# Edge features of two node groups in one pass of TensorE's two row halves, in a graph network of eight layers on one core

## The chip, the core and the metric

The kernel runs on one core of a Trainium2 chip. A core has five engines with an instruction stream each: TensorE (PE in the profile, with its weight loads as PEld) multiplies matrices into PSUM, VectorE (DVE) and ScalarE (ACT) work element by element and can read and write PSUM, GpSimd (POOL) issues the indirect DMAs that gather and scatter rows, and SyncE (SP) issues most other DMAs. The engines run side by side and wait for each other through semaphores. The metric is the device time of one execution in microseconds (us); lower is better.

## The reference

The graph has 3125 nodes with 256 features and 50000 edges, sorted by receiver `dst`; everything is fp32. Eight layers follow each other, each added onto x: four of them work on the graph, four are feed-forward networks (FFN). The change touches mostly the work that the kernel does in one loop for the first three:

```python
# layer 0, graph: a weight matrix of 256x256 for each of 16 edge types
msg = einsum('ni,rio->rno', layernorm(x), weight)[edge_type, src] * edge_weight1
x = x + segment_sum(msg, dst)
# layer 0, FFN: 8 experts, gelu, weighted by the top 2 of a router; all tokens
x = x + moe(layernorm(x))
# layer 1, graph
cut = 0.5 * (cos(edge_weight * pi / 5) + 1) * (edge_weight < 5)
W   = (edge_attr_64 @ W_dist + b_dist) * cut[:, None]        # 64 -> 256
agg = segment_sum(embed_table[node_type][src] * W, dst)
x = x + concat([layernorm(x), agg]) @ W_comb + b_comb
```

After that come an FFN on the highest-scored rows (layer 1), a graph layer with attention over the edges and an FFN with 16 experts, top 2 (layer 2), and a graph layer with a maximum over the edges and an FFN with 8 experts, top 2 (layer 3).

## The kernel before

**The loop over tiles, `stage_one`.** Receivers are taken in 25 tiles of 126 nodes, a tile in 21 groups of 6 nodes (the last tile in 17), 521 groups in all. As the edges are sorted, the edges of a group are a run of at most 128 consecutive ones, and a group's work has the edges on the 128 partitions. `window(k)` (L874) does one group:

- `rows[k]` holds for each edge the sender's normalized row and its embedding, 512 columns, gathered by POOL (`fetch_rows`, nine buffers `g`).
- Two matmuls sum the first half by node and edge type (L881, into `c`): the right side is `s0`, 128 edges by 96 = 6 nodes x 16 types, one-hot times the edge's weight, built by DVE (L866). ACT copies `c` into `aT` for every second group (L885).
- One matmul makes the edge filter (L888, into `pw`): the left side is `feats[k]`, 65 rows by 128 edges, loaded by SP (`fetch_feats`, a row of ones and the 64 features, from a table laid out that way); the right side `wd` has `b_dist` in row 0 and `W_dist` in the other 64.
- DVE multiplies `pw` with the embedding half of the row (L891) into `mt`. Then the next row gather is issued.

`build` (L859) also makes `s1` (L868): for each edge its receiver's place in the tile as a one-hot, 32 wide or 128 wide, times the cutoff. `add_up(t, b)` (L896) multiplies `s1` with `mt` into `agg`, for three batches of groups: in the first two, four groups at a time go to four blocks of 32 columns of TensorE (L907). Groups run in the order of the batches, so that batch 0 ends with group 17, batch 1 with 19 and batch 2 with 10; batches 0 and 1 are summed a few groups later, batch 2 after the tile's groups.

After the groups a tile has eight steps of `weigh` (L915): in each, `aT` of two edge types times their 256x256 weights, added up in PSUM (`f`); the last adds the result to x. After each group and each `weigh` step comes a slot, `between()` (L1140): it issues one step of the `flows` (the FFN of layer 0 and the rest of layer 1 for a pair of finished tiles), one of the `background`, and one load of late weights (on ACT's DMA queue) and one zero fill (on SP's).

**The background** is a Python generator: each `yield` ends a step. It prepares, beside the loop, tables for it and for later layers. `begin(t)` (L1211) finds where the groups of tiles t and t+1 start among the edges: `find.fetch` gathers rows, and two slots later `starts` (L647) counts in them (DVE, `find.count`, L586) and multiplies the counts (PE, L651). Further on the edge features are reduced to an attention term (`b_at`, L1276, 100 loads), and nodes are ranked by degree, one tile after the other: `chosen(t)` makes a one-hot on DVE (L1325) for matmuls (L1347), a second loop (L1371 to L1377) places the ranked nodes by one-hots `k_sel` and `k_ohh`. Steps of the background are taken in every slot for the first 116 slots, in every third after that.

**Order.** The stages are under `manual_schedule`: each engine takes its instructions in the order in which the program issues them. PSUM in the loop has two banks for `c`, two halves-of-banks `pw`, one each for `agg` and `f`, and two `w` for flows and background.

**The experts of layers 2 and 3** (class `Experts`) are laid out by a planner, `Plan` (L1685): each job is a generator that yields the engine, an estimated duration and what it waits for, and the planner orders the issues by estimated times. `loads` (L1978) is the job of SP's loads: for each chunk of tokens and each expert, first the tokens `x` (two buffers; it waits until the chunk's rows have been scattered, `self.sent`), then the two blocks of weights (rings of `W_BUFS` = 2 buffers). `run` (L1999) does the expert's matmuls. In layer 2 the gathers of the graph layer use nine buffers `g_rows` before.

## Time and profile before

| | us |
|---|---|
| median of 7 runs | 3792.72 |
| lowest and highest run | 3787.91, 3804.38 |
| the profiled execution, its own time | 3798.97 |
| its span, first to last instruction | 3797.3 |
| loop over tiles, `stage_one` | 99 to 1716 |
| layer 2, gathers of the attention layer | 2028 to 2646 |
| layer 2, experts, last chunk | 2684 to 2816 |
| layer 3, gathers | 2880 to 3390 |
| layer 3, experts | 3445 to 3797 |

A page of the profile is of one execution: busy time by engine, the span in 40 slices (each digit the busy share in tenths; PEclk the granted TensorE clock in tenths of full speed), the DMA queues, the chain that ended last, and the costliest groups of instructions. A group's line reads: code line, engine, operation, output<-inputs, shapes, xcount | busy us, mean ns of one | idle time of the engine just before them, and the instructions that ended most of it. A line of waits reads: who waited <- for whom: us in total, times, longest. In a timeline a line stands for several passes of one kind: start, time from the first start to the last end, engine, line, operation, xcount. An fp32 matmul shows as two passes. Tiles of the loop end at 178.0, 271.3, 345.0, 423.9, 480.8, 535.6, ... 1715.7 us; from the fifth on most odd tiles take 54.9 us, tiles 12 and 13 together 188.7.

### The profile page before, as it was taken

What the parts mean: (1) busy time and instruction counts of PE and PEld (TensorE: products, weight loads), DVE (VectorE), ACT (ScalarE), POOL (GpSimd) and SP (SyncE); (2) the same over time, 40 slices, a digit from 0 to 9 for tenths busy, and PEclk for the clock granted to TensorE, in tenths of its full rate; (3) what the DMA queues carried; (4) which work ended last, traced back from release to release, by engine and by line L of the source; (5) the groups of instructions that cost most, each with busy time, mean ns of one, the idle gap of its engine ahead of it and who ended that gap; (6) DMA issues with size and microseconds to landing.
All of it is one profiled execution on the core that took longest, in us unless ns stands there. A gap on an engine that the chain in (4) does not pass through costs nothing. (4 is left out here: it accounts for less than half of the span.)

```text
span 3797.3 us, 46833 instructions
## 1 busy us (share of the span) xinstructions
PE 2632.4 (69%) x13015; PEld 2108.9 (56%) x13015; DVE 1962.7 (52%) x7555; ACT 851.2 (22%) x1821; POOL 1722.2 (45%) x1971
## 2 busy tenths in 40 slices
PE   3778899999899999998492228568562112238994
PEld 2556788877677888886371117356451112226673
DVE  4445666666566555554334665656663333346311
ACT  2112232322122233232120113123230000014331
POOL 0342343352154343320125777777346777753333
PEclk9967999999899999999595559779785555557997
DMA  5756654553243454430213348677543333324563
GB/s 178 235 156 210 179 145 133 155 163 88 68 127 109 115 151 122 116 110 26 92 56 88 103 115 274 178 217 235 169 154 86 105 105 105 105 80 139 158 213 96
DMA packets 274481, 518.32 MB, mean 136 GB/s; under 512 B 53069, under 2 KB 176107, under 8 KB 274195
## 3 DMA queue, kind: packets, MB, share of 16 engines
q0 software_dynamic: 103744, 303.34, 27.3%
q1 hardware_dynamic: 159598, 201.27, 17.4%
q10 hardware_dynamic: 10852, 10.45, 0.9%
q8 instruction: 113, 1.85, 0.2%
q14 instruction: 174, 1.42, 0.1%
HBM read 428.07 MB, written 86.78 MB: 136 GB/s over the span
## 5 line engine op out<-in xcount | busy, mean ns | idle before, releaser
L136 POOL DMA_INDIRECT g<-tab,m_si x521 | 496.3, 953 | 953.0 <-DVE mt L891 503.8
L136 POOL DMA_INDIRECT g_rows<-tab,srcI x413 | 402.9, 976 | 130.9 <-issue 102.7
L136 POOL DMA_INDIRECT g_row<-tab,srcI x413 | 390.7, 946 | 131.3 <-issue 119.7
L881 PEld LDWEIGHTS c<-s,g 128*128 128x128 f32 x2084 | 343.9, 215 | 124.0 <-issue 45.4
L881 PE MATMUL c<-s,g 128*128 128x96 f32 x2084 | 350.7, 296 | 65.0 <-DMA g<-tab,m_si 21.6
L920 PE MATMUL f<-w_rel,aT 128*126 128x256 f32 x1600 | 380.9, 389 | 0.0
L888 PE MATMUL pw<-w_d,f 65*128 65x256 f32 x1042 | 370.2, 440 | 0.0
L885 ACT COPY aT<-c 128x384 f32<-128x384 f32 (+1 forms) x323 | 237.7, 736 | 572.2 <-PE c L881 552.2
L2368 DVE TENSOR_TENSOR ACC<-ACC,g_row 128x256 f32<-128x256 f32 x413 | 175.6, 425 | 340.4 <-DMA g_row<-tab,srcI 340.2
L920 PEld LDWEIGHTS f<-w_rel,aT 128*126 128x126 f32 x1600 | 305.2, 193 | 52.1 <-issue 4.3
L1643 PE MATMUL tp<-ident,ACC 128*128 128x128 f32 x50 | 16.6, 435 | 420.8 <-DVE ACC L2368 420.8
L1973 PE MATMUL mm<-ro_xt,ro_w 128*128 128x192 f32 (+3 forms) x1152 | 268.8, 382 | 48.6 <-ACT ro_h L2038 23.6
L891 DVE TENSOR_TENSOR mt<-pw,g 128x256 f32<-128x256 f32 x521 | 218.2, 419 | 95.7 <-PE pw L888 94.6
L1977 PE MATMUL y<-ro_w,ro_h 128*96 128x256 f32 (+2 forms) x1152 | 265.9, 383 | 0.0
L1973 PEld LDWEIGHTS mm<-ro_xt,ro_w 128*128 128x128 f32 x1152 | 202.5, 208 | 98.2 <-ACT ro_h L2038 32.2
L1643 PEld LDWEIGHTS tp<-ident,ACC 128*128 128x128 f32 x50 | 7.2, 204 | 428.3 <-issue 353.2
L1977 PEld LDWEIGHTS y<-ro_w,ro_h 128*96 128x96 f32 (+2 forms) x1152 | 199.3, 178 | 42.9 <-issue 1.0
L1038 PE MATMUL w<-w,b_h 128*126 128x256 f32 x800 | 217.2, 396 | 5.5 <-ACT xt L951 4.5
L1029 PE MATMUL w<-xt,w 128*128 128x252 f32 (+1 forms) x832 | 212.1, 379 | 3.0 <-ACT b_h L1031 1.3
L2248 DVE SCALAR_TENSOR_TENSOR ACC<-g_rows,g_e,ACC 128x256 f32<-128x256 f32 x413 | 201.2, 487 | 13.6
L1040 DVE SCALAR_TENSOR_TENSOR x<-w,b_comb,x 126x256 f32<-126x256 f32 x200 | 96.0, 480 | 173.4 <-PE w L1038 172.6
L140 POOL DMA_INDIRECT xg<-XX,ro_pos x100 | 101.1, 1011 | 176.5 <-issue 75.4
(582 smaller groups left out, 4623.7 us busy)
## 6 DMA issues: line engine op xcount, KB each, us to landing
ro_w<-in_L_ffn_blocks SPq DMA_DIRECT2D x72, 514.0 KB
ro_w<-in_L_ffn_blocks SPq DMA_DIRECT2D x72, 512.0 KB
f<-in_attr_t SPq DMA_DIRECT2D x521, 32.5 KB
xg<-zero SPq DMA_DIRECT2D x78, 200.0 KB
b_at<-in_edge_attr SPq DMA_DIRECT2D x100, 125.0 KB
tabr<-v SPq DMA_DIRECT2D x12, 758.0 KB
g<-tab,m_si POOLq DMA_INDIRECT x521
g_rows<-tab,srcI POOLq DMA_INDIRECT x413
```

The source lines that it names most:

```text
L136: return nc.gpsimd.indirect_dma_start(out=dst, out_offset=None, in_=table, in_offset=bass.IndirectOffsetOnAxis(ap=idx, axis=0))
L881: nc.tensor.matmul(pc[:, h, o : o + GW], g[:, h * P : (h + 1) * P], sums[k][0], start=True, stop=True)
L885: nc.scalar.copy(aT[:, :, :, b : b + n * GN].rearrange("p k r n -> p k n r"), pc[:, :, : n * GW].rearrange("p k (n r) -> p k n r", r=16))
L888: nc.tensor.matmul(pw, feats.pop(k), wd, start=True, stop=True)
L891: nc.vector.tensor_tensor(mt[0], pw, rows.pop(k)[:, D:], op=OP.mult)
L920: nc.tensor.matmul(cur["f"][:TN], aT[:, h, r, :], wrel[:, h, r, :], start=(r == 0 and h == 0), stop=(r == 15 and h == 1))
L1029: nc.tensor.matmul(ph, w["01"][:, e, k, i * P : (i + 1) * P], xt[:, k, : n * TN], start=(k == 0), stop=(k == 1))
L1038: nc.tensor.matmul(py, last[:, k, i * TN : (i + 1) * TN], w["02"][:, e - 1, k, :], start=(k == 0), stop=(k == 1))
L1973: nc.tensor.matmul(ph, w[:, o : o + P], xt[:, k, :], start=(k == 0), stop=(k == 1))
L1977: nc.tensor.matmul(py, h[:, i, s], w[:, i * D : (i + 1) * D], start=(i == 0), stop=(i == self.fc - 1))
L2248: stt(u, g[:, r, :D], e[:, r0 + r : r0 + r + 1], u, op0=OP.mult, op1=OP.add)
L2368: nc.vector.tensor_tensor(u, u, rows.pop(r), op=OP.max)
```

## The change

- The groups of a tile are taken in pairs, in their order; the last of a tile stands alone. A tile `f` holds the features of two groups, 64 rows each in the two halves of the partitions, and `wd` holds `W_dist` twice. When the second group's `c` is issued, the two filter matmuls follow each other, each with 64 rows of its own half. `F_BUFS` is 4 pairs, no longer 6 groups.
- The bias is `bd`, `b_dist` on all partitions. `seed()` makes ACT copy it into a PSUM bank `pw` (three banks now) ahead of the matmul, which adds to it. The first three seeds are ahead of the loop and have a matmul with the identity as well.
- The cutoff is multiplied in DVE's product, which becomes a `scalar_tensor_tensor`. One-hots without it are made by `whose(t, b)` for a batch at a time: for batches 0 and 1 in two instructions of four groups each (at groups 4 and 15), for batch 2 in five (at group 10, ahead of its `window`).
- `agg` and `f` share one PSUM bank, `af`. The third `add_up` comes in the first slot after the groups; `weigh` takes the other seven, with two or three edge types each.
- In the background, `find.count` has a step of its own ahead of `starts`; the one-hots of the ranking are made one item ahead of PE.
- In `Experts`, `loads` becomes `tokens` and `weights`, two jobs for the planner; in layer 2 the weights of the last chunk's experts from the third on go into the gathers' buffers, after the last of the gathers.
- The path for groups with too many edges (`beyond`) is adapted, and an unused tile (`lg2`) goes. Both are left out below, as are the planner's lines that only carry the new names.

```diff
@@ -86,7 +86,7 @@
-G_BUFS, F_BUFS = 9, 6
+G_BUFS, F_BUFS = 9, 4
@@ -366,7 +366,8 @@
-    wd = wb.tile([65, D], F32, name="w_d")
+    wd = wb.tile([P, D], F32, name="w_d")
+    bd = wb.tile([P, D], F32, name="b_d")
@@ -410,8 +411,9 @@
-    nc.scalar.dma_start(wd[0:1, :], a["L1_gnn_b_dist"])
-    nc.scalar.dma_start(wd[1:65, :], a["L1_gnn_W_dist"])
+    for i in range(2):
+        nc.scalar.dma_start(wd[64 * i : 64 * i + 64, :], a["L1_gnn_W_dist"])
+    nc.scalar.dma_start(bd, bass.AP(tensor=a["L1_gnn_b_dist"].tensor, offset=a["L1_gnn_b_dist"].offset, ap=[[0, P], [1, D]]))
@@ -646,8 +648,6 @@
     def starts(t, n, pf):
-        for i in range(t, t + n):
-            find.count(i)
@@ -673,6 +673,8 @@
+            for t in range(2):
+                find.count(t)
@@ -832,9 +834,17 @@
-        rows, feats, sums = {}, {}, {}
-        agg_of = {}
-        nxt = {"g": 0, "f": 0, "s": 0}
+        pairs, half_of = [], {}
+        for k, (t, j) in enumerate(wins):
+            if pairs and len(pairs[-1]) == 1 and wins[pairs[-1][0]][0] == t:
+                pairs[-1].append(k)
+            else:
+                pairs.append([k])
+            half_of[k] = len(pairs) - 1, len(pairs[-1]) - 1
+        rows, feats, sums, seeds = {}, {}, {}, []
+        nxt = {"g": 0, "f": 0, "s": 0, "d": 0}
@@ -846,12 +856,25 @@
+            if k < len(pairs):
+                nxt["f"] += 1
+                feats[k] = eb.tile([P, P], F32, name="f", bufs=F_BUFS)
+                for i, w_ in enumerate(pairs[k]):
+                    t, j = wins[w_]
+                    v = nc.values_load(mixI[j : j + 1, t : t + 1], engines={EN.SP}, min_val=0, max_val=E)
+                    nc.sync.dma_start(feats[k][64 * i : 64 * i + 64, :], a["attr_t"][:, bass.ds(v, P)])
+        def seed():
+            k = nxt["d"]
             if k < len(wins):
-                nxt["f"] += 1
-                t, j = wins[k]
-                feats[k] = eb.tile([65, P], F32, name="f", bufs=F_BUFS)
-                v = nc.values_load(mixI[j : j + 1, t : t + 1], engines={EN.SP}, min_val=0, max_val=E)
-                nc.sync.dma_start(feats[k], a["attr_t"][:, bass.ds(v, P)])
+                nxt["d"] += 1
+                pw = ps("pw", [P, 2, D])[:, 0, :]
+                if k < 3:
+                    nc.tensor.matmul(pw, ident, bd, start=True, stop=True)
+                nc.scalar.copy(pw, bd)
+                seeds.append(pw)
@@ -860,14 +883,9 @@
-                a = quarter(j)
-                a, m1 = (0, P) if a is None else (32 * a, 32)
-                s1 = eb.tile([P, m1], F32, name=f"s1_{m1}", bufs=13 if m1 == 32 else 3)
-                nc.vector.tensor_scalar(s1, iota_f[:, a : a + m1], m[:, F_DST, j : j + 1], m[:, F_CUT, j : j + 1],
-                                        op0=OP.is_equal, op1=OP.mult)
-                sums[k] = s0, s1
+                sums[k] = s0
@@ -878,33 +896,64 @@
-                nc.tensor.matmul(pc[:, h, o : o + GW], g[:, h * P : (h + 1) * P], sums[k][0], start=True, stop=True)
+                nc.tensor.matmul(pc[:, h, o : o + GW], g[:, h * P : (h + 1) * P], sums[k], start=True, stop=True)
-            pw = ps("pw", [P, D])
-            nc.tensor.matmul(pw, feats.pop(k), wd, start=True, stop=True)
+            del sums[k]
+            q, i = half_of[k]
+            if i + 1 < len(pairs[q]):
+                return
+            ft = feats.pop(q)
+            pws = [seeds.pop(0) for _ in pairs[q]]
+            for i, pw in enumerate(pws):
+                v = slice(64 * i, 64 * i + 64)
+                nc.tensor.matmul(pw, ft[v, :], wd[v, :], start=False, stop=True, skip_group_check=True)
-            mt = mults[t, j] = eb.tile([P, D], F32, name="mt", bufs=11), sums.pop(k)[1]
-            nc.vector.tensor_tensor(mt[0], pw, rows.pop(k)[:, D:], op=OP.mult)
-            fetch_rows()
-        ag_of, mults = {}, {}
+            for k, pw in zip(pairs[q], pws):
+                t, j = wins[k]
+                mt = mults[t, j] = eb.tile([P, D], F32, name="mt", bufs=11)
+                stt(mt, pw, mts[t][:, F_CUT, j : j + 1], rows.pop(k)[:, D:], op0=OP.mult, op1=OP.mult)
+                seed()
+                fetch_rows()
+        ag_of, mults, ones_of = {}, {}, {}
+        def whose(t, b):
+            m = mts[t][:, F_DST]
+            n = GL if t == NT - 1 else GC
+            for js in together[b]:
+                js = [j for j in js if j < n]
+                if b < 2:
+                    s1 = eb.tile([P, 4, 32], F32, name="s1g", bufs=3)
+                    of = m[:, js[0] : js[-1] + 1 : 5].unsqueeze(2).to_broadcast([P, len(js), 32])
+                    nc.vector.tensor_tensor(s1[:, : len(js)], iota_f.rearrange("p (q n) -> p q n", n=32)[:, : len(js)],
+                                            of, op=OP.is_equal)
+                    for i, j in enumerate(js):
+                        ones_of[t, j] = s1[:, i, :]
+                    continue
+                for j in js:
+                    q = quarter(j)
+                    n1 = P if q is None else 32
+                    s1 = ones_of[t, j] = eb.tile([P, n1], F32, name=f"s1_{n1}", bufs=2 if q is None else 3)
+                    o = 32 * (q or 0)
+                    nc.vector.tensor_scalar(s1, iota_f[:, o : o + n1], m[:, j : j + 1], None, op0=OP.is_equal)
         def add_up(t, b):
             if b == 0:
-                cur["agg"] = ps("agg", [P, D])
+                cur["agg"] = ps("af", [P, 2, D])[:, 0, :]
             for js in together[b]:
-                    a = quarter(j)
-                    mt, s1 = mults.pop((t, j))
-                    o = agg if a is None else agg[32 * a : 32 * a + 32]
-                    nc.tensor.matmul(o, s1, mt, start=not begun, stop=(j == 10), skip_group_check=True)
+                    q = quarter(j)
+                    o = agg if q is None else agg[32 * q : 32 * q + 32]
+                    nc.tensor.matmul(o, ones_of.pop((t, j)), mults.pop((t, j)), start=not begun, stop=(j == 10),
+                                     skip_group_check=True)
@@ -913,9 +962,9 @@
-            if i == 0:
-                cur["f"] = ps("f0", [P, D])
-            for r in (2 * i, 2 * i + 1):
+            if i == 1:
+                cur["f"] = ps("af", [P, 2, D])[:, 0, :]
+            for r in range(16 * (i - 1) // 7, 16 * i // 7):
@@ -1152,6 +1201,8 @@
+        for _ in range(3):
+            seed()
@@ -1161,6 +1212,8 @@
+                if wins[k][1] in (4, 15, 10):
+                    whose(t, (4, 15, 10).index(wins[k][1]))
@@ -1180,9 +1233,10 @@
             for i in range(8):
-                weigh(t, i)
-                if i == 1:
+                if i == 0:
+                else:
+                    weigh(t, i)
@@ -1213,6 +1267,9 @@
+            yield
+            for i in range(t, t + n):
+                find.count(i)
@@ -1341,8 +1398,9 @@
+        nxt = chosen(0)
         for t in range(NT):
-            sel = chosen(t)
+            sel, nxt = nxt, (chosen(t + 1) if t + 1 < NT else None)
@@ -1365,15 +1423,21 @@
+        def both(t):
+            ohl = eb.tile([P, P], F32, name="k_sel")
+            ohh = eb.tile([P, 3, NT], F32, name="k_ohh")
+            nc.vector.tensor_scalar(ohl, iota_f, lo[:, t : t + 1], None, op0=OP.is_equal)
+            for i in range(3):
+                nc.vector.tensor_scalar(ohh[:, i, :], iota_f[:, :NT], hi[:, t : t + 1], val[:, t, i : i + 1],
+                                        op0=OP.is_equal, op1=OP.mult)
+            return ohl, ohh
+        nxt = both(0)
+        yield
             for t in range(t0, t0 + 5):
-                ohl = eb.tile([P, P], F32, name="k_sel")
-                ohh = eb.tile([P, 3, NT], F32, name="k_ohh")
-                nc.vector.tensor_scalar(ohl, iota_f, lo[:, t : t + 1], None, op0=OP.is_equal)
-                for i in range(3):
-                    nc.vector.tensor_scalar(ohh[:, i, :], iota_f[:, :NT], hi[:, t : t + 1], val[:, t, i : i + 1],
-                                            op0=OP.is_equal, op1=OP.mult)
+                (ohl, ohh), nxt = nxt, (both(t + 1) if t + 1 < NT else None)
@@ -1423,7 +1487,7 @@
-            tc.tile_pool(name="eb", bufs=2) as eb, psums(c0=2, pw=2, agg=1, f0=1, w=2):
+            tc.tile_pool(name="eb", bufs=2) as eb, psums(c0=2, pw=3, af=1, w=2):
@@ -1976,25 +2040,38 @@
-        def loads(self):
-            pool, half = self.pool, 2 * self.f + self.fc
+        def tokens(self):
-                    r0 = e * m * k
+                    r0, at = e * m * k, c * self.n + e
-                    xfree = self.XR.take()
-                    x = pool.tile([P, self.bk, D], F32, name="ro_x", bufs=2)[:m, :k]
+                    free = self.XR.take()
+                    x = self.pool.tile([P, self.bk, D], F32, name="ro_x", bufs=2)[:m, :k]
-                    parts = [(x, plan[0].moved(f, m * k * 1024), xfree)]
-                    for i, ring in enumerate(self.W):
-                        f = yield "SP", 0.45, (ring,)
-                        wfree = ring.take()
-                        w = pool.tile([P, half if i == 0 else self.fc * D], F32, name=f"ro_w{i}", bufs=W_BUFS)
-                        nc.sync.dma_start(w, self.blocks[e * P : (e + 1) * P, half * i : half + i * self.fc * D])
-                        parts.append((w, plan[0].moved(f, 0.53e6), wfree))
-                    self.there.append(parts)
-                    self.came[len(self.there) - 1].t = f
+                    self.there[at] = x, plan[0].moved(f, m * k * 1024), free
+                    self.came[at].t = f
+        def weights(self, more=None):
+            half = 2 * self.f + self.fc
+            for c in range(len(self.chunks)):
+                for e in range(self.n):
+                    for i in range(2):
+                        n = (half, self.fc * D)[i]
+                        if more and c + 1 == len(self.chunks) and e >= W_BUFS:
+                            ring, make, since = more
+                            f = yield "SP", 0.45, (ring, since)
+                            w = make()[:, :n]
+                        else:
+                            ring = self.W[i]
+                            f = yield "SP", 0.45, (ring,)
+                            w = self.pool.tile([P, n], F32, name=f"ro_w{i}", bufs=W_BUFS)
+                        free = ring.take()
+                        nc.sync.dma_start(w, self.blocks[e * P : (e + 1) * P, half * i : half * i + n])
+                        at = (c * self.n + e) * 2 + i
+                        self.loaded[at] = w, plan[0].moved(f, 0.53e6), free
+                        self.fetched[at].t = f
@@ -2306,7 +2386,9 @@
-            pl.add(0, ex2.loads())
+            pl.add(0, ex2.tokens())
+            pl.add(0, ex2.weights((blocks, lambda: gp.tile([P, GB, ZW], F32, name="g_rows", bufs=GR_BUFS)
+                                   .rearrange("p r d -> p (r d)"), here[order2[-1]])))
@@ -2469,9 +2552,8 @@
-    f = np.zeros((65, EPAD), np.float32)
-    f[0, :E] = 1.0
-    f[1:, :E] = given["edge_attr_64"].T
+    f = np.zeros((64, EPAD), np.float32)
+    f[:, :E] = given["edge_attr_64"].T
```

## The prediction

> **What bounds the kernel now.** I read the page's totals and its 40 slices first, then busy time by stretch, then groups, PE's waits and single passes. The page:
>
> ```profile
> span 3797.3 us, 46833 instructions
> PE 2632.4 (69%) x13015; PEld 2108.9 (56%) x13015; DVE 1962.7 (52%) x7555; ACT 851.2 (22%) x1821; POOL 1722.2 (45%) x1971
> PE   3778899999899999998492228568562112238994
> PEclk9967999999899999999595559779785555557997
> ```
>
> A slice is 95 us. PE is full from slice 5 to slice 18 and nearly idle in the gather stages (2028 to 2646, 2880 to 3390 us), which POOL bounds and the change leaves alone. The tile loop is 99 to 1716 us. By stretch (length, then PE, PEld, DVE, ACT and POOL busy, granted clock, DMA share, GB/s):
>
> ```profile
> 178.00:271.00 93.00, 63.98 (x249) 48.53 (x250) 37.26 (x146) 9.91 (x14) 38.49 (x41) 0.60 0.53 151
> 896.00:1085.00 189.00, 172.12 (x853) 138.05 (x853) 113.88 (x508) 35.05 (x64) 48.49 (x51) 0.86 0.28 78
> 1085.00:1716.00 631.00, 613.62 (x3519) 514.66 (x3517) 368.45 (x1529) 187.04 (x349) 235.57 (x272) 0.98 0.43 121
> 2660.00:2680.00 20.00, 7.36 (x23) 4.46 (x23) 12.86 (x71) 2.55 (x7) 1.10 (x3) 0.50 0.00 0
> 2684.00:2816.00 132.00, 104.95 (x547) 86.30 (x548) 87.08 (x320) 47.86 (x138) 56.60 (x71) 0.88 0.65 213
> ```
>
> The reader sees two kinds of time. In 1085 to 1716 PE is 97% busy: only less PE work helps. Elsewhere PE has gaps, and a gap costs twice, as the clock sits near half behind it. The tile loop's gaps are named by PE's waits in 90 to 1720 us (total, times, longest):
>
> ```profile
> PE w L651 <- DVE startF L586: 35.6, 10, 5.7
> PE c L881 <- DMA g<-tab,m_si: 21.6, 1, 21.6
> PE c L881 <- DVE s L866: 19.4, 20, 2.6
> PE w L1377 <- DVE k_ohh L1375: 10.1, 17, 2.6
> ```
>
> **The change part by part.** The sum goes against the profiled execution: 3798.97 us, a span of 3797.3 and 1.7 around it. That is 6.25 us above the median of the runs, 3792.72; I take the sum off both alike.
>
> *Pairs on PE.* Single passes (start, us, instructions), from three stretches:
>
> ```profile
> 1302.51 0.62 PE L888 MATMUL pw<-w_d,f 65*128 65x256 f32 x2
> 1302.97 0.58 PE L881 MATMUL c<-s,g 128*128 128x96 f32 x4
> ...
> 1338.97 0.62 PE L888 MATMUL pw<-w_d,f 65*128 65x256 f32 x2
> 1339.53 1.07 PE L907 MATMUL agg<-mt,s 128*32 128x256 f32 x16
> 1340.53 1.13 PE L1038 MATMUL w<-w,b_h 128*126 128x256 f32 x4
> ...
> 1135.39 1.12 PE L1012 MATMUL w<-w_b,b_ct 8*126 8x256 f32 x4
> 1136.44 0.91 PE L920 MATMUL f<-w_rel,aT 128*126 128x256 f32 x3
> ```
>
> pw costs 1302.97 − 1302.51 = 0.46 us: two passes, 0.23 each. Two of them cost 0.92. L907 shows that parts of the array do work side by side: 16 passes of 32 columns in 1.00 us, where 16 × 0.23 would be 3.7. L1012 shows what a change to few rows and back costs: four passes take 1.05 us, not 4 × 0.216 = 0.86, so 0.19; the pass before it also runs 0.10 long in such places (L888 ahead of L907: 0.56, not 0.46). Together about 0.29 beside the passes, with a first weight load exposed some 0.39. A pair side by side: 2 × 0.216 + 0.39 = 0.82, against 0.92: −0.10 × 248 pairs = −24. A tile's 21 groups leave one unpaired: 0.82 against 0.46, +0.36 × 25 = +9. I take −14. Upper end: the halves run one after the other, 4 × 0.216 + 0.39 = 1.25, +0.33 × 248 + 9 = +91. No row here has two halves of rows, so both ends stay; I side with L907, the only row in which parts of the array meet.
> The Trainium skill (TensorEngine Tiling (Array Packing), section Theoretical Speedup) allows up to 2× at 64 rows; by that alone 248 pairs would save 0.46 each, −114 us, and the sum below would be −171. The same page, section PSUM Bottleneck, speaks against the change: packing speeds up TensorE, not the emptying of PSUM, which here grows by a seed and a longer product a group; were that the limit, the pairs would give nothing and the sum be −57. L891's product, 0.419 us in slots of 1.75, does not show that limit before the change.
>
> *Bias.* 521 copies of 128×256 by ACT into PSUM. Nearest rows: from PSUM 0.37, between SBUF tiles 0.51:
>
> ```profile
> L2055 ACT COPY ro_y<-y 128x256 f32<-128x256 f32 x32 | 11.8, 370 | 35.9 <-PE y L1977 34.6 <-issue 1.3
> L2218 ACT ACTIVATE g_u<-XX,hasnt 128x256 f32<-128x256 f32 x25 | 12.7, 510 | 0.0
> L2248 DVE SCALAR_TENSOR_TENSOR ACC<-g_rows,g_e,ACC 128x256 f32<-128x256 f32 x413 | 201.2, 487 | 13.6
> ```
>
> That is 193 to 266 us on an engine 30% busy in 1085 to 1716; it rises to some 45%. The new wait: ACT holds a seed until DVE has read that bank, and behind it in ACT's order stand the copy of c and the flows' ACT steps. With three banks, a pair's loop is 0.2 + two products 0.98 + a seed 0.5, 1.7 us, against two slots of 1.75 us: covered, at nothing. If the cover goes (ACT behind a DMA issue, or a product late), each pair pays up to some 0.2: +50.
>
> *Cutoff and one-hots, DVE.* Removed: L868, 147.6 + 17.1 = 164.7 us. Added: 100 four-wide comparisons at L1331's 0.295, 30; 74 narrow and 50 wide at 0.313 and 0.343, 40; 521 products 0.487 instead of 0.419, 35. Net −60 us on an engine 58% busy, off the path; it may shorten the 19.4 us of L866's waits, which I leave as a bound. But before group 10's product stand s0 and five one-hots, 1.6 us, and the sum over the last groups moves from after four relations to the first slot, so that PE meets a product not ready: 0 to 0.5 us a tile, and the bank shared by sums and `f` makes the first relations wait for ACT's 0.37 copy, behind a flow step except in the early tiles. +6 (0 to +20). Steady part with the pairs: −14 + 6 = −8. Its ends: −34 (−15 with no stall, and L866's 19.4 gone) and +111 (+91 + 20; the +50 of uncovered seeds is not added there, as a slower PE gives them cover).
>
> *f and wd loads.* SP still issues 521 loads, of 64 rows for 65. One load of bias more on ACT's queue ahead of the loop; nothing. POOL's gathers now leave in twos, nine buffers deep, and POOL waits 503.8 us for buffers already: nothing.
>
> *Background.* `find.count` runs a slot ahead of the matmul in `starts`, so the 35.6 us over ten waits (L651) go; what is late next is the same DVE work behind other PE work, and the edge loads, twelve steps later, fall out of the phase that steps every slot. Also, 178 to 271 us runs at clock 0.60 where PE's work is 64 of 93 us. Fewer gaps help there, but DMA carries half of its time and tile 0's first gathers (21.6) are untouched; ACT's weight loads hold up c's copies by 12.3 us there and now seeds too. Ends: −65 (35.6 and the half-clock share of 30) to +5. I take −28. Thirteen added steps end a sequence that finished at 1214 us, 500 before the loop: nothing. In 896 to 1085 the one-hots made one item ahead remove L1377's 10.1 and its like, and part of the half clock: 17 us of gaps there; −15 (−30 to 0).
>
> *Level-2 and level-3 experts.* In 2660 to 2680 DMA moves 0 GB/s: weights stand in SP's queue behind token loads that wait for the scatter. Split, they are loaded then, and the last chunk uses the idle gather buffers. PE's gaps in 2684 to 2816 are 132 − 105 = 27 us, of which some 21 name weights and tokens; the tokens' own load stays. Next in line are the stores of the outputs and the fixed tail to 2880. −16 (−35 to +5). In the last level the gaps mostly follow routing: −4 (−10 to +5).
>
> Sum: −8 − 28 − 15 − 16 − 4 = −71: 3728 for a profiled execution like this one, 3722 for the median.
>
> **The rivals.**
> *Halves one after the other* (slower). For it: no row shows two row halves together. Against it: L907. Price: +91 in place of −14, with the +6 and the other moves' −63: +34, 3827. It decides from where what the other moves bring is eaten: (63 − 9 − 6)/248, 0.19 us a pair more than two old products.
> *ACT becomes the late engine.* Seeds and products wait for each other and pairs pay 0.2: +50. For it: one in-order ACT queue with DMA issues in it. Against it: 30% busy. −71 + 50: 3772.
> *The gaps close altogether.* 178 to 424 us runs at full clock (−65) and the L2 experts become PE-bound (−35), lookahead −30: −130, 3662 or so. For it: the clock in 424 to 896 is 0.97 wherever PE has no gaps. Against it: the other waits there (gathers, b_at) stay.
> *Nothing that shows.* The background's waits turn into waits on the same DVE work one slot later and the pairs' gain is eaten by unpaired groups: 3793.
>
> **How the numbers follow.** As summed 0.52 (own range 3685 to 3765); gaps closed 0.13; ACT late 0.16; halves in turn 0.13; nothing 0.06. A measurement of this kernel tells about 0.2%, 7.6 us, from no change. Faster: 0.52 + 0.13 + 0.15 of ACT late = 0.80; same: 0.04; slower: 0.13 + 0.03 of nothing = 0.16. The range 3642 to 3812 takes in the first three and part of the fourth, leaving out some 0.15. Predicted: the likeliest, 3722.
>
> **What would show it.** *Pairs:* the step from a pair's first pass to the next c near 0.8 us (side by side) or 1.25 (in turn). *Bias:* the seeds' group near 370 to 510 ns, idle ahead of it named by DVE's product, and no wait of PE on ACT. *One-hots:* L868 gone, DVE down by some 60 us. *Background:* no wait of `starts` on startF, the stretch 178 to 271 shorter by 15 or more. *Lookahead:* tiles 12 and 13, 188.7 us now, near 174. *Experts:* weights on the DMA in 2660 to 2680, the stretch to the end of the experts shorter by 16. The prediction is wrong if odd tiles in 1085 to 1716, 54.9 us now, are longer than 57, or if c waits for ACT's copies.

## The result and the profile after

The changed kernel takes 3805.91 us (median of 15 runs, 3801.57 to 3810.31), beside 3792.05 for the kernel before (36 runs): a ratio of 1.0035, interval 1.0026 to 1.0044. It is 13.9 us slower. Forecast were 3722 us, a gain of 71, with 3642 to 3812 as the range and 0.16 for slower. The time lies inside the range and the direction was wrong. One run of `split_only`, a kernel described below, took 4525.6 us at a granted clock of 0.60; it belongs to a slower state and is left out of that kernel's ratio.

The profiled execution took 3797.28 us, with a span of 3795.4. That is 8.6 us under the median of its kernel, and the profiled execution of before was 6.9 us over its own. Set against each other the two traces show the changed kernel 1.7 us faster, while the runs say 13.9 slower. The traces are used for where time goes, the runs for how much it is.

The page of the changed kernel:

```profile
span 3795.4 us, 46667 instructions
PE 2616.4 (69%) x13021; PEld 2019.7 (53%) x13021; DVE 1923.3 (51%) x7257; ACT 1031.6 (27%) x2343; POOL 1727.8 (46%) x1971
PE   3777899989989999998493228658682112238994
PEclk9867999999989999999596558769685555557997
```

The work moved as reckoned in kind: DVE is 39 us less busy (60 were reckoned from the removed and added lines), ACT 180 more, PE 16 less. The same stretches as before, after the change (length, PE, PEld, DVE, ACT, POOL, granted clock, DMA share, GB/s):

```profile
178.00:271.00 93.00, 64.85 (x285) 46.19 (x286) 39.11 (x155) 22.84 (x44) 41.01 (x44) 0.65 0.58 168
896.00:1085.00 189.00, 169.60 (x894) 130.50 (x894) 119.58 (x509) 56.80 (x121) 55.86 (x59) 0.92 0.35 97
1085.00:1716.00 631.00, 599.27 (x3453) 468.80 (x3452) 359.74 (x1455) 255.49 (x559) 238.02 (x272) 0.98 0.42 118
2660.00:2680.00 20.00, 6.12 (x13) 2.53 (x13) 17.04 (x58) 2.26 (x7) 9.31 (x16) 0.50 0.71 249
2684.00:2816.00 132.00, 106.45 (x547) 85.93 (x547) 89.42 (x346) 49.01 (x140) 59.00 (x74) 0.86 0.50 163
```

DMA now carries 249 GB/s in 2660 to 2680 where it carried none: the weights do come early. But the tile loop ends 12 us later (its last `weigh` matmul at 1727.3, before at 1715.2), and in 1085 to 1716 PE is less busy in the same time. PE's waits in 90 to 1720 us show where it stands:

```profile
PE af L955 <- DVE s1g L933: 36.6, 26, 5.1
PE c L899 <- DVE s L886: 31.1, 33, 4.5
PE w L651 <- DVE startF L588: 30.5, 9, 8.4
PE c L899 <- DMA f<-in_attr_t: 18.8, 1, 18.8
PE af L955 <- DVE s L943: 15.6, 11, 7.5
PE w L1441 <- DVE k_ohh L1431: 10.9, 18, 2.7
PE w L1078 <- ACT xt L1000: 8.2, 9, 1.2
```

Two of these lines are new: the sums (L955) wait 36.6 + 15.6 = 52 us for one-hots, those of four groups (L933) and those of batch 2 (L943). Before, the sums waited 5.9 us in all. And two lines that were to go are still there: `starts` waits 30.5 us (35.6 before), the ranking 10.9 (10.1 before). The wait of `c` for the other one-hots, `s0` (L886), which the prediction hoped to see shorter, has grown from 19.4 to 31.1 us, and the FFN's matmuls wait 9.1 us for a copy by ACT, `xt` (8.2 of them at L1078; 4.1 before).

The tiles' ends (us, with the tile's length), from the last `weigh` matmul of each. The third and fourth pairs of columns are the kernels `bg_only` and `early_onehots`, described below:

```
tile      before          after        bg_only   early_onehots
  3    417.3  75.8    413.3  90.6    394.0  76.0    409.7  85.9
 11    895.8  60.0    899.8  65.8    863.3  61.4    883.5  65.0
 14   1149.2  64.7   1154.0  96.0   1120.9 103.2   1138.9  97.5
 17   1323.7  54.9   1335.7  60.3   1295.4  57.5   1317.5  60.3
 24   1715.2  51.4   1727.3  52.5   1685.9  51.4   1706.1  51.0
```

### The profile page after: what moved, and what is told of

It is laid out like the page before. It is cut to its first block, busy times and chain, and to the rows that moved or that the text cites. A ratio compares the mean times of both kernels' runs of the same rounds, so it can differ in the third digit from the quotient of the medians.

```text
span 3795.4 us, 46667 instructions
## 1 busy us (share of the span) xinstructions
PE 2616.4 (69%) x13021; PEld 2019.7 (53%) x13021; DVE 1923.3 (51%) x7257; ACT 1031.6 (27%) x2343; POOL 1727.8 (46%) x1971
## 5 line engine op out<-in xcount | busy, mean ns | idle before, releaser
L899 PEld LDWEIGHTS c<-s,g 128*128 128x128 f32 x2084 | 315.9, 210 | 126.6 <-issue 55.6
L899 PE MATMUL c<-s,g 128*128 128x96 f32 x2084 | 339.8, 297 | 60.3 <-DVE s L886 31.1
L969 PE MATMUL af<-w_rel,aT 128*126 128x256 f32 x1600 | 370.3, 383 | 6.5 <-ACT ag L962 6.5
L969 PEld LDWEIGHTS af<-w_rel,aT 128*126 128x126 f32 x1600 | 299.6, 189 | 59.9 <-ACT ag L962 13.1
L918 DVE SCALAR_TENSOR_TENSOR mt<-pw,m_mt,g 128x256 f32<-128x256 f32 x521 | 228.3, 477 | 97.4 <-PE pw L913 96.5
L876 ACT COPY pw<-b_d 128x256 f32<-128x256 f32 x521 | 197.1, 383 | 283.5 <-DVE mt L918 273.2
L2037 PE MATMUL mm<-ro_xt,ro_w 128*128 128x192 f32 (+3 forms) x928 | 234.0, 402 | 29.6 <-ACT ro_h L2118 24.1
L2041 PE MATMUL y<-ro_w,ro_h 128*96 128x256 f32 (+2 forms) x1040 | 245.6, 390 | 0.0
L1078 PE MATMUL w<-xt,w 128*128 128x252 f32 (+1 forms) x832 | 219.4, 388 | 11.4 <-ACT xt L1000 8.2
L913 PE MATMUL pw<-w_d,f 64*128 64x256 f32 x1042 | 221.4, 471 | 0.8 <-ACT pw L876 0.8
L2037 PEld LDWEIGHTS mm<-ro_xt,ro_w 128*128 128x128 f32 x928 | 171.7, 207 | 75.1 <-ACT ro_h L2118 30.8
L2041 PEld LDWEIGHTS y<-ro_w,ro_h 128*96 128x96 f32 (+2 forms) x1040 | 182.4, 180 | 42.9 <-issue 1.3
```

What stands on the lines that cost most here:

```text
L876: nc.scalar.copy(pw, bd)
L899: nc.tensor.matmul(pc[:, h, o : o + GW], g[:, h * P : (h + 1) * P], sums[k], start=True, stop=True)
L913: nc.tensor.matmul(pw, ft[v, :], wd[v, :], start=False, stop=True, skip_group_check=True)
L918: stt(mt, pw, mts[t][:, F_CUT, j : j + 1], rows.pop(k)[:, D:], op0=OP.mult, op1=OP.mult)
L969: nc.tensor.matmul(cur["f"][:TN], aT[:, h, r, :], wrel[:, h, r, :], start=(r == 0 and h == 0), stop=(r == 15 and h == 1))
L1078: nc.tensor.matmul(ph, w["01"][:, e, k, i * P : (i + 1) * P], xt[:, k, : n * TN], start=(k == 0), stop=(k == 1))
```

## The experiments

The kernels were run in groups; those of a group share a chip and the runs of before. In the runs of the result and in three groups (chips 12, 9 and 3 of the record) before took 3791 to 3795 us; in two others (chips 8 and 7) it took 4284 and 4254. The first are called the faster chips here, the last two the slower chips. Runs on the slower chips are given with the ratio to their own before and are told apart.

### The three parts alone

Three kernels are the kernel before with one part of the change each: `split_only` has `tokens` and `weights` in place of `loads`; `loop_only` the tile loop's part; `bg_only` the background's two.

> The kernel before with one part of the change alone: the experts' loads split into tokens and weights (and the last chunk's weights in the gathers' buffers). Theory A, that this part gives what the profile after shows between 2646 and 2880 us: 10 to 16 us faster than before, 3776 to 3782. Rival B, that the gain there is an accident of the one profiled execution: within 4 us of 3792.

> The kernel before with the tile loop's part alone: pairs, seeds, cutoff in the product, one-hots by batch, shared bank; background and experts' loads as before. Theory A, that the loop's part costs, since PE waits for one-hots (52 us of waits named in the profile after) against 8 us won on the pairs: 10 to 25 us slower than before, 3802 to 3817. Rival B, that the pairs' gain and the waits cancel and the loss lies in the background's steps: within 5 us of 3792.

> The kernel before with the background's part alone: the count one step ahead and the one-hots of the ranking one item ahead. Theory A, that waits only change their names, as DVE is the late one with the same work: within 8 us of 3792 either way. Rival B, the prediction's sum for these two terms: 43 us faster, 3749. Rival C, that the steps added push later work into denser tiles: 8 to 15 us slower.

Before: 3790.96. `split_only`: 3776.45, ratio 0.9958 (0.9944 to 0.9973), 14.5 us faster. `bg_only`: 3776.47, ratio 0.9957 (0.9942 to 0.9973), also 14.5 faster. `loop_only`: 3824.03, ratio 1.0087 (1.0069 to 1.0105), 33 us slower. So the headline part costs and the two beside it gain. My expectation of nothing for the background was a miss: it gains, though not the 43 us of the prediction. The three sum to +4 us, the whole is +13.9. The 10 us between them are no more than the four intervals leave open (3 to 7 us each way), so that it isn't shown that anything arises only when the parts meet.

### The one-hots

In `own_onehots` each group's one-hot is built by itself two groups ahead, as before the change; in `early_onehots` the batches stay and are only issued earlier:

```diff
-                if wins[k][1] in (4, 15, 10):
-                    whose(t, (4, 15, 10).index(wins[k][1]))
+                if wins[k][1] in (16, 14, 15):
+                    whose(t, (16, 14, 15).index(wins[k][1]))
                 window(k)
```

> The kernel after with each group's receiver one-hot built alone and two groups ahead, as before the change, but without the cutoff; 521 instructions of DVE in place of 174. Theory A, that the batches' late one-hots cost the loop its pairs' gain: 10 to 25 us faster than the kernel after, 3781 to 3796, with the sums' waits on one-hots gone. Rival B, that DVE's time itself is what counts: 40 to 60 us more of DVE work make it 5 to 15 us slower than the kernel after, 3811 to 3821.

> The kernel after with the one-hots of each batch issued three to four groups earlier in DVE's order (batch 0 at the seventh group and no longer the tenth, batch 1 at the fourteenth and no longer the eighteenth, batch 2 at the eighteenth and no longer the last); same instructions. Theory A, that what costs is the slack, one slot between a batch's one-hots and the sum that needs them when DVE stands behind a DMA: at least as fast as with one-hots of each group, 3778 to 3790. Rival B, that the bunches themselves cost: 3800 to 3808.

`own_onehots`: 3788.23, ratio 0.9992 (0.998 to 1.0004), 17.7 us under the changed kernel. `early_onehots`: 3767.72 against a before of 3792.29, ratio 0.993 (0.9907 to 0.9952), 38.2 us under the changed kernel with the same instructions. That settles the largest cause: not the number of the one-hots, their place. What the 20 us between the two kernels are is not settled: `own_onehots` has 297 instructions more on DVE (521 one-hots in place of 224; the 174 of its expectation is a miscount), 37 us of busy time in the traces. PE's waits in `early_onehots`, the same view:

```profile
PE c L899 <- DVE s L886: 35.6, 35, 4.0
PE w L651 <- DVE startF L588: 31.1, 9, 8.0
PE c L899 <- DMA f<-in_attr_t: 18.7, 1, 18.7
PE af L955 <- DVE mt L918: 10.3, 6, 6.8
```

The sums' waits on one-hots are gone; 10.3 us on products are left. How a one-hot can come to be late shows in the timeline of the changed kernel around 376 us (start, us, instruction, idle before and what ended it). VectorE:

```profile
374.63 0.87 DVE L918 SCALAR_TENSOR_TENSOR mt<-pw,m_mt,g 128x256 f32<-128x256 f32 x2
377.47 0.42 DVE L1333 TENSOR_TENSOR b_at<-b_at,b_a 125x256 f32<-125x256 f32 x1 [1.97 <-DMA b_at<-in_edge_attr]
...
380.73 0.42 DVE L1333 TENSOR_TENSOR b_at<-b_at,b_a 125x256 f32<-125x256 f32 x1 [2.14 <-DMA b_at<-in_edge_attr]
...
381.76 0.49 DVE L933 TENSOR_TENSOR s1g<-iota_f,m_mt 128x128 f32<-128x128 f32 x2
382.16 0.87 DVE L918 SCALAR_TENSOR_TENSOR mt<-pw,m_mt,g 128x256 f32<-128x256 f32 x2
```

and TensorE:

```profile
375.88 1.23 PE L913 MATMUL pw<-w_d,f 64*128 64x256 f32 x4
382.10 1.94 PE L955 MATMUL af<-mt,s1g 128*32 128x256 f32 x16 [4.99 <-DVE s1g L933]
```

VectorE, in its order, stands twice behind a load of edge features for the background (1.97 and 2.14 us). The one-hots, 0.49 us of work, are queued behind that, and the sum that needs them is next on TensorE: 4.99 us idle. The granted clock of 320 to 395 us is 0.73, and 0.84 before. This is one of the longest of the 37 waits. Taken one by one in the trace, nine of the 37 (31.3 of the 52.2 us) hold a stop of VectorE for a DMA, 14.5 us in all; in the other 28 (20.9 us) it is busy throughout with what stands ahead in its order: the group's `s0`, the one-hots themselves, steps of the FFN and the background. Over all 37 VectorE is busy for 36.8 us.

Before the change each one-hot was issued two groups ahead of its own group, for the last group of a batch five groups ahead of the sum. The change left one group for batches 0 and 1 (`whose`, then `window`, then `add_up`, all in the same pass of the loop) and one group and a slot for batch 2. `early_onehots` gives four to five groups.

### The pairs and the bias

`rows65` is the changed kernel with the filter matmul as before, 65 rows for one group, and neither seeds nor pairs; `no_seed` keeps the pairs and leaves the bias out.

```diff
-            pws = [seeds.pop(0) for _ in pairs[q]]
...
-                nc.tensor.matmul(pw, ft[v, :], wd[v, :], start=False, stop=True, skip_group_check=True)
+            pw = ps("pw", [P, 2, D])[:, 0, :]
+            nc.tensor.matmul(pw, feats.pop(k), wd, start=True, stop=True)
```

> The kernel after with the filter matmul as before, one group at a time on 65 rows with the bias in them, without seeds or pairs, and all the rest of after: cutoff in the product, one-hots by batch, sums in the first slot and in the bank shared with f. Theory A, that pairs and seeds give PE 8 us and cost nothing, the one-hots being the loss: 3806 to 3822. Rival B, that a pair's second half comes too late for DVE, so that products bunch and PE waits where DVE is late: 3780 to 3795.

> The kernel after without the bias: no copies by ACT into PSUM, the paired matmuls start their sums themselves, three banks as after. It leaves out b_dist. Theory A, that seeds are covered: 3800 to 3808. Rival B, that ACT's 197 us of seeds and their wait for DVE's product hold up the copies of c and the FFN's steps: 3780 to 3795.

`rows65`: 3819.64, ratio 1.0063 (1.004 to 1.0085): 13.7 us more than the changed kernel by the medians, 10.6 by the ratios, with an interval of some 9 us each way. So pairs with their seeds gain about what was forecast (14). `no_seed`: 3798.90, ratio 1.0017 (1.0004 to 1.0031): the seeds cost 7 us by the medians, where nothing was forecast; the intervals of the two kernels overlap a little.

The traces agree where the background is over: tiles 18 to 23 take 340.0 us before, 339.1 in the changed kernel, 337.7 in `early_onehots`, 346.2 in `rows65` and 335.2 in `no_seed`. There the steady loop does about what the prediction said of it (8 us less in 25 tiles, 1.9 in six). But `rows65` stands 6.0 us there for late one-hots, the changed kernel 1.0, so that what `rows65` loses is not all the filter's.

Passes of one pair in the changed kernel:

```profile
1523.05 0.58 PE L899 MATMUL c<-s,g 128*128 128x96 f32 x4
1523.56 0.70 PE L913 MATMUL pw<-w_d,f 64*128 64x256 f32 x4
1524.19 0.48 PE L1118 MATMUL w<-w_c,at 128*126 128x256 f32 x1
```

The two halves start 7 ns apart (single records at 1523.561 and 1523.568, then 1523.881 and 1523.888): side by side. From the first to the next line 0.63 us, as each of the two steps takes 0.32 and 0.31 where a pass takes 0.216 elsewhere; with 0.09 ahead of it and 0.10 behind, where neighbouring passes are stretched (0.205 for 0.112 and 0.318 for 0.216), the pair takes 0.83. Forecast was 0.82. A group that stands alone has the same 0.205, 0.32 and 0.31.

The groups of the product, the filter and the seeds:

```profile
L918 DVE SCALAR_TENSOR_TENSOR mt<-pw,m_mt,g 128x256 f32<-128x256 f32 x521 | 228.3, 477 | 97.4 <-PE pw L913 96.5
L913 PE MATMUL pw<-w_d,f 64*128 64x256 f32 x1042 | 221.4, 471 | 0.8 <-ACT pw L876 0.8
L876 ACT COPY pw<-b_d 128x256 f32<-128x256 f32 x521 | 197.1, 383 | 283.5 <-DVE mt L918 273.2 <-issue 4.7 <-DVE s L943 2.1
```

A seed takes 383 ns, at the low end of the two rows it was bounded by. PE waits 0.8 us in all for seeds. The 7 us of `no_seed` are not in that wait. They are about the size of another: PE's wait for ACT's copy `xt` in the FFN is 9.1 us in the changed kernel, 0.9 in `no_seed` and 4.1 in `rows65`, which has neither pairs nor seeds. This fits a seed that waits for its product (273 us of ACT's waits) and holds up what stands behind it in ACT's order.

### Without the headline

> The kernel after without its headline: the tile loop as before, the background's and the experts' parts as after. If the two parts add up (14.5 and 14.5 us faster alone): 3762, between 3756 and 3769. Rival, that both only use the same idle time of DMA or a common shift of the clock: 3774 to 3780.

`no_pairs`: 3766.07, ratio 0.9923 (0.9901 to 0.9945). The two parts add to within 4 us of what they bring alone. With early one-hots (3767.72) the whole change is 1.7 us from it, within the intervals of both. Once the one-hots are early, the paired loop neither gains nor loses that a run could tell. One cost that it keeps is plain in the traces of the faster chips: PE waits for `s0` 30.3 to 37.5 us in every kernel with pairs (35.6 in `early_onehots`) and 17.2 to 19.5 in every kernel without (19.0 in `no_pairs`, 17.2 in `rows65`, which has the rest of the change).

### The ranking, the count and three further edits, on the slower chips

`look_only` and `count_only` are the kernel before with one half of the background's part. `early_s0`, `apart_early` and `early_count` are `early_onehots` with s0 built a group earlier; with banks and the third sum as before and two seeded banks; and with one more step between gather and count.

> The kernel before with only the ranking's one-hots made one item ahead (and the step that this adds). The prediction's term: 15 us faster, 3777, with PE's waits on k_ohh (10.1 us) gone. Rival, from the profile after, where that wait is 10.9 us: DVE makes one-hots for five items in one step, PE waits for their making and not for their place in the order, so nothing: within 4 us of 3792.

> The kernel early_onehots with the other one-hots, s0, built three groups ahead and no longer two (five buffers). If slack on DVE's order is what the paired loop still lacks (35.6 us of PE's waits for c name s0): 8 to 20 us faster than early_onehots, 3748 to 3760. Rival, that PE then stops at the next thing that DVE owes, the products and their banks: 3764 to 3770.

> The kernel early_onehots with the sums and f in a bank each again, the third sum after four relations and eight steps of weigh as before, and two seeded banks in place of three. If the shared bank and the sum in the first slot cost (6.5 us of waits on the copy, 10.3 on products): 6 to 15 us faster than early_onehots, 3753 to 3762. Rival, that the third seeded bank is worth as much: 3765 to 3785.

> The kernel early_onehots with one more step of the background between the gather of rows and their count. If DVE's stop at the count is for the gathered rows (35.7 us of DVE's waits in the profile after, in 12 places) and holds up products and one-hots: 8 to 20 us faster than early_onehots, 3748 to 3760. Rival, that the stop only moves to the loads of edge features, which come next in the background: 3764 to 3771.

On this chip before took 4283.93 us, so that none of the times expected can be compared. `look_only`: 4270.40, ratio 0.9963 (0.9946 to 0.9979). `early_s0`: 4332.06, 1.0103 (1.0074 to 1.0133). `apart_early`: 4340.40, 1.0141 (1.0111 to 1.017). `early_count`: 4356.08, 1.0164 (1.0136 to 1.0192). Three were run again, beside the count alone:

> The kernel before with only the count of rows one step ahead of its matmul. If the 14.5 us of the whole background part are in the first four tiles, where the profile of bg_only ends 23 us earlier: 10 to 18 us faster than before. Rival: they are in the ranking: within 4 us.

> The kernel look_only once more, since the kernel before took 4284 us on the chip of its call and 3791 elsewhere. If the ranking's one-hots are worth nothing where PE waits for their making: within 4 us of before. The first look had them 0.37% faster: if that holds, 10 to 18 us.

> The kernel apart_early once more, for the same reason. Where before takes 3791 us, early_onehots took 3768. If the shared bank and the sum in the first slot cost: 3753 to 3762; if the third seeded bank is worth as much: 3765 to 3785.

> The kernel early_s0 once more, for the same reason. If slack for s0 is what the paired loop still lacks: 3748 to 3760; if PE then stops at the next thing that DVE owes: 3764 to 3770. If the kernel before takes 4284 us again, the paired loop is 1% slower than before again.

Again a slower chip, before 4253.84. `count_only`: 4239.63, 0.9964 (0.9948 to 0.998). `look_again`: 4243.80, 0.9972 (0.9956 to 0.9988). `apart_again`: 4300.46, 1.0117 (1.009 to 1.0144). `s0_again`: 4288.65, 1.0084 (1.0055 to 1.0113). Here count and ranking gain alike, 14 and 10 to 13.5 us. That the ranking would bring nothing was a miss, though PE's wait for `k_ohh` stands at 9.6 us in `look_again` as it did without it. How the 14.5 us of `bg_only` divide on the faster chips was not measured by runs. In the traces tile 3, long before the ranking, ends at 394.0 in `bg_only`, 395.6 and 395.9 in the two of `no_pairs`, and at 414.7 in `split_only`, whose loop is that of before: some 20 us are there by then.

The paired loop with early one-hots, 0.7% faster than before on a faster chip, is with one of these further edits 0.8 to 1.6% slower than before on the slower ones. PE's waits of `s0_again` in 90 to 1860 us:

```profile
PE pw L913 <- ACT pw L876: 40.4, 30, 4.6
PE w L651 <- DVE startF L588: 27.8, 7, 8.7
PE c L899 <- issue: 25.6, 9, 19.0
PE af L969 <- ACT ag L962: 12.3, 10, 5.0
```

The first line is the prediction's second rival: PE waits 40.4 us for seeds, 0.8 in the changed kernel on a faster chip, and a seed still takes its 376 ns there (the median). With two seeded banks (`apart_again`) it is 45.9. ACT itself is held by nothing that the profile names (35 us of "issue" ahead of seeds). This wait alone doesn't explain the loss: in `early_count`, the slowest of these kernels, it is 6.4 us, and there PE waits 58.5 for `s0`.

`s0` a group earlier does in the traces what it was to do, 6.9 us of waits for it in both runs against 35.6 in `early_onehots` on the faster chip. Whether that shortens the time was not settled, as `early_onehots` itself never ran on a slower chip. For the same reason neither the banks nor the later count can be priced: `apart_early` and `apart_again` are slower than `early_s0` and `s0_again`, but within the intervals, and differ from them in more than one thing. `early_count` is slower than `early_s0` beyond the intervals (4356 against 4332).

### The last two

> The kernel after once more, beside the next one. Where before takes 3791 us, after takes 3806 and should do so again, within 5 us. Where before takes some 4260 us, the paired loop with early one-hots was 0.8 to 1.4% slower than before; if late one-hots cost there as elsewhere, the kernel after is 1.5 to 2.5% slower; if another cost rules there, 0.8 to 1.4%.

> The kernel no_pairs once more, on the chip of the run above: the change without its headline. If the background's and the experts' parts hold on any chip: 0.6 to 1.0% faster than before, as in the first run (0.77%). If they lean on the one chip: within 0.3%.

On a chip with before at 3795.21: the changed kernel 3804.62, ratio 1.0026 (1.001 to 1.0042), and `nopairs_again` 3765.44, ratio 0.9917 (0.9892 to 0.9942). Both hold. The kernel to keep is the one without pairs: the background's and the experts' parts, 0.8% faster than before. The changed kernel itself and this version were not run on the slower chips.

## Why the prediction was wrong

Terms of the sum, as forecast and as measured (us, from the medians):

| term | forecast | measured | by |
|---|---|---|---|
| pairs with seeds | −14 | −13.7 | `rows65` to the changed kernel |
| one-hots before the sums | +6 (0 to +20) | +38.2 | changed kernel to `early_onehots` |
| background, with ranking | −43 | −14.5 | `bg_only` |
| experts, both layers | −20 | −14.5 | `split_only` |
| not forecast | | +18 | the rest to +13.9 |

**The step that failed: the one-hots.** The prediction weighed DVE's work (−60 us, "off the path") and gave the new order 0 to 0.5 us a tile, for the five one-hots of batch 2 alone. The four-wide ones of batches 0 and 1 were costed as work and not placed. They cost most: 36.6 us of PE's waits in 26 places against 15.6 in 11. The wait is not the half microsecond of the one-hots; it is all that DVE, in its order, has still ahead of them, work (36.8 of the 52.2 us) and stops for a DMA (14.5), up to 5.1 us at once at L933. 74.7 us of DVE's waits name the `b_at` loads in the profile after. That row was in the trace before as well, 68.1 us, and PE waited for no receiver one-hot while these stood groups ahead. What a reader could have done: count, for each thing DVE makes, the groups between its issue and its reader, before and after, and set them beside the longest stretch of work and stops ahead of it. (The 1.6 us that the prediction puts ahead of group 10's product are its five one-hots alone by its own rows; with `s0` it is 2.0. The measured cost doesn't hang on it.)

**The background.** The forecast took `starts`' wait for DVE as a wait for the count's place in the order. After the change it is 30.5 us of 35.6, and DVE's own waits point to why: 35.7 us of them end with the gathered rows that the count reads (20.9 before). A step earlier, the count waits for its DMA and holds DVE with it. There is a gain all the same: in `bg_only` tile 3 ends 23 us earlier than before in the traces (20.7 earlier than in `split_only`, whose loop is that of before), and the runs give 14.5 for the whole part; 28 for the count alone was too much. Since the wait that was to go is still 28.1 us in `bg_only`, what the gain comes from was not found. For the ranking, 17 us of gaps were credited. PE still waits 10.9 us for `k_ohh`: five items are made and used in one step, four instructions of DVE to one matmul, so that PE follows DVE whichever item is ahead; this is read from the code. In the traces tiles 12 to 14 take 253.4 us before and 254.2 after, and the ranking's last part (`k_ohh`) moved from 985 to 1038 us to 1074 to 1128. On the slower chips the same edit gained 10 to 13.5 us, so it is not idle; what of it counts was not found.

**The pairs.** The mechanism was right: side by side, 0.83 us a pair, which with the unpaired groups is 248 × 0.09 less 25 × 0.36, about 13 us. The prediction's 0.39 beside the passes comes out as 0.09 and 0.10 in the passes beside it and 0.20 in the pair's own; that the last is a weight load was not shown. The rule of the Trainium skill that was weighed there (TensorEngine Tiling (Array Packing), section Theoretical Speedup, up to 2× at 64 rows) would have had 0.46 us off each pair; measured is 0.09. That the runs then give −13.7 for pairs and seeds together is in part luck: the seeds, put at nothing, cost some 7, the waits for `s0` grew, which had no term, and the interval is wide.

**The experts.** Right in kind: DMA at 249 GB/s where it was at 0, and 14.5 us of 20. In the traces the last use of a gathered row and the last expert matmul of layer 2 stand at 2661.7 and 2815.9 us before, at 2673.8 and 2811.2 after: 154 and 137 us, 17 less, where 16 were forecast. Layer 3 gave about 1 and not 4 (`split_only` against before, 927.5 and 928.5 us from layer 3's first work on VectorE to the end).

**The rest.** Between `no_pairs` and the changed kernel lie 39.8 us: −13.7 and +38.2 are 24.5 of them. Some 15 are left (18 in the table, as the two side parts together bring 26 and not 29), of which the seeds' 7 are no part, as these are inside the −13.7. The intervals of the kernels compared (3 to 9 us each way) leave room for much of it to be noise. The traces put it early: tile 3 ends at 395.6 in `no_pairs` and at 409.7 in `early_onehots`, while tiles 12 to 24 take 832.2 and 822.6. In tile 3 DVE stands behind the `b_at` loads for 31.7 and 42.0 us, and the granted clock is 0.89 and 0.78. The pairs alone don't explain it, as tile 3 takes 85.8 us in `rows65` too, with late one-hots in their place (85.9 in `early_onehots`, 76.9 in `no_pairs`). A kernel without pairs and with early one-hots would tell; it was not run, and the cause stays open.

**The rivals.** Halves in turn: excluded by the 7 ns. ACT late: on the faster chips worth the seeds' 7 us and not 50; on the slower ones PE does wait for seeds, 40 to 48 us in four of the five runs. Of the two signs of being wrong, odd tiles past 57 us came in two of the five from tile 15 on (58.1 and 60.3), and no wait of `c` for ACT's copies is named. The likeliest case missed because its three gains were each taken near what the waits' names promised, and its one loss near zero.

## What to carry to other kernels

What an instruction costs that is moved later in an engine's order is not its length; it is what stands ahead of it there, work and stops for a DMA, as soon as its reader stands closer than that. So list the distance from maker to reader for every operand of the busy engine, and keep it when work is batched: three changed numbers in the program were worth 38 us here. And a wait that names an engine goes only if what that engine waits for goes too.

## What the runs showed of the hardware

- Two fp32 matmuls of 64 rows in the two halves of the rows start 6 to 7 ns apart and run together, onto two PSUM banks. The passes beside such a pair are 0.09 and 0.10 us longer, and its own two steps take 0.32 and 0.31 us where a pass takes 0.216 elsewhere, so that a pair of 256-column filters takes 0.83 us against 0.92 for two of 65 rows.
- ACT copies 128×256 from SBUF into PSUM in 383 ns; from SBUF into SBUF ACTIVATE took 510 in the trace before.
- The kernel before took 3791 to 3795 us on some chips and 4254 to 4284 on others. In the traces of before (faster) and `look_only` (slower) the durations of single instructions are the same (the row gather 953 and 958 ns, the sender sums 296 and 299), the loop ends 62 us later and the whole 457; ACT's idle time that the profile gives no named cause ("issue" or "remote") is 49 us in the first and 967 in the second, DVE's 8 and 463. What makes the difference was not found. The paired loop with early one-hots gained 0.7% on a chip of the first kind; with one further edit each, three kernels lost 0.8 to 1.6% on chips of the second.
